# Weight combinations of a seven-product projection on VectorE instead of GpSimd

## The chip, the cores and the metric

The kernel runs on one core of a Trainium2 chip. The metric is the device time of one execution in microseconds (us). The engines that matter are TensorE (PE, matrix products; PEld is its loading of weights), VectorE (DVE), ScalarE (ACT), GpSimd (POOL) and SyncE (SP, which here issues the DMA transfers). Each engine works through its own instructions in a fixed order, and they meet at semaphores.

## What is computed

Two batches of 1024 tokens with 1024 channels pass through four layers: causal attention with rotary positions and an adapter prefix (32 heads of 32), a feed-forward layer with routed low-rank experts, a second attention (8 heads of 16), and the feed-forward layer again. Only the projections of the first attention are touched by the change:

```python
def _L0_attn_a_ref(x, w_attn, w_proj, adapter_wte, gating):
    qkv = jnp.einsum('btc,oc->bto', x, w_attn)
    q, k, v = jnp.split(qkv, 3, axis=-1)
    ...
    q = _apply_rope(q, cos, sin)
    k = _apply_rope(k, cos, sin)
    scores = jnp.einsum('bhqd,bhkd->bhqk', q, k) / jnp.sqrt(jnp.asarray(hd, x.dtype))
    scores = jnp.where(causal, scores, jnp.asarray(-jnp.inf, x.dtype))
    attn = jax.nn.softmax(scores, axis=-1)
    y = jnp.einsum('bhqk,bhkd->bhqd', attn, v)
    ...
x = L0_attn_a_x
x = x + _L0_attn_a_ref(_layernorm(x, axis=-1), L0_attn_a_w_attn, L0_attn_a_w_proj, L0_attn_a_adapter_wte, L0_attn_a_gating)
x = x + _L0_ffn_ref(_layernorm(x, axis=-1), ...)
x = x + _L0_attn_b_ref(_layernorm(x, axis=-1), ...)
x = x + _L0_ffn_ref(_layernorm(x, axis=-1), ...)
```

## The kernel before

**Stages.** Stage A (`stage_a`) holds the first attention for both batches and takes the first half of the time; after it come the output projection, the feed-forward layers and the second attention, which the change leaves alone. In stage A the heads are taken in eight groups of four. `attend` walks through rounds: in each round PE writes one double bank of scores (`sc`, line L304), one double bank of transposed scores (`st`, L372 and L374), products with v (L396), and then a portion of filler work. VectorE finds each row's minimum of the negated scores in a custom instruction with a read of its accumulator (L317), ScalarE forms the exponentials (L325, L485), GpSimd masks the diagonal (L381). The two double banks take turns, so PE's next scores need VectorE to be done with the last ones.

**Filler.** The class `Filler` holds generators of PE work, above all the projections of the coming groups, and puts them between the rounds. It also has a list of chores, small jobs for other engines. After each portion of PE work it runs one chore; `flush` runs all that are left at once. Running a chore means that its instruction is placed at this point of its engine's order. PE and GpSimd follow the order in which the program is written; on VectorE the instructions marked with `keep_in_program_order` do (`pin_sub`, `pin_add` among them).

**Seven products.** For all groups but the first of each batch, `project_blocks` makes k and q of a group with seven block products instead of eight (`seven`), and `values` does the same for v of two groups, half at a time. The rows of the normalized input and of the weights are each cut into two by two blocks. The seven products need sums and differences of blocks:

- of the input, once a batch: `combine` stores three of them in DRAM (`td`, streamed back as `tt`), `combine_first` changes one block in place;
- of the weights, for every set: `factors` makes s1 = w21 + w22, s2 = s1 - w11 and w21 = w11 - w21 (chores, L629), `last_factor` w12 - s2 (chores, L635). Each is 128x512 elements and is done by GpSimd in two pieces of 128x256.

In `seven` the products come in the order 1, 6, 2, 7, 5, 4, 3. Product 6 uses s2, product 7 the changed w21, product 5 s1 and the changed input block, product 3 the last combination. `first` and `settled` are `rotate` for k and q: a shuffle and a product on VectorE (L795, L796), then four instructions on GpSimd (L799, L800). Before product 6 and before product 3 the whole list of chores is flushed. The last combination's chores are put on the list behind product 5.

There are 14 such sets for k and q (groups 1 to 7 of two batches; tiles `wqk`, `s`) and 7 for v (`wv`, `s_v`). A set of k and q is begun at the end of the projection before (`begin`), a set of v in the middle of an even group (`begin_values`, at the `None` that `seven` yields). For the first value set of batch 1 this isn't so: it is begun at the head of `values`, right in front of its own product 1, behind the chores of `combine_first` and of the k and q set of group 1.

Of the kernel before, what the change touches and what calls it, by code (L numbers as in the profile page):

```python
# [21 lines left out]
B, T, C = 2, 1024, 1024  # L22
# [26 lines left out]
class Filler:  # L49
# [10 lines left out]
        self.ahead = 0  # L60
        self.chores = deque()

    def flush(self):
        while self.chores:
            self.chores.popleft()()

    def add(self, gen, gate=None):
        self.gens.append((gen, gate))
# [1 line left out]
    def step(self, cold=True):  # L70
        while self.gens:
            g, gate = at = self.gens[0]
            if gate is not None and gate not in self.done:
                return None
            if not cold and isinstance(g, Dense) and not g.ready:

                g.prepare()
                return None
            try:
                r = next(g)  # L80
            except StopIteration:
                self.gens.remove(at)
                self.ahead = 0
                continue
            if r is WAIT:
                return None
            if r is AHEAD:
                self.ahead += 1
                self.prepare(1)
                continue  # L90
            if isinstance(r, tuple):
                self.done.add(r)
                self.at[r] = self.spent
                continue
            self.spent += r
            if self.chores:
                self.chores.popleft()()
            return r
        return None

# [43 lines left out]
def tile_model(ctx: ExitStack, tc: tile.TileContext, d, out: bass.AP):  # L144
    nc = tc.nc
    pe, dve, act, pool, sp = nc.tensor, nc.vector, nc.scalar, nc.gpsimd, nc.sync
# [3 lines left out]
    fill = Filler()  # L150
# [8 lines left out]
    def block_bank(shape, name, i=0):  # L159
        return ps.tile(shape, F32, tag=pair[i], name=name)  # L160
# [363 lines left out]
    def stage_a(wk, big):  # L524
# [58 lines left out]
        def in_pieces(op):  # L583
            def both(dst, x, y):
                for h in range(0, HF, 2 * P):
                    op(dst[:, h : h + 2 * P], x[:, h : h + 2 * P], y[:, h : h + 2 * P])
            return both

        def pin_sub(*a):
            tc.keep_in_program_order(dve.tensor_sub(*a))  # L590
# [4 lines left out]
        def made(ts, b, i, c, op, x, y):  # L595
            t = ts[i, c] = big.tile([P, HF], F32, tag="tt", name=f"tn{b}_{i}_{c}")
            op(t, x, y)
            sp.dma_start(td[b, i, c], t)

        def combine(b):  # L600

            ts = {}
            for c in range(4):
                b11, b12, b21, b22 = (block(b, i)[:, c, :] for i in (11, 12, 21, 22))
                fill.chores.append(lambda c=c, x=b22, y=b12: made(ts, b, 3, c, pin_sub, x, y))
                fill.chores.append(lambda c=c, y=b11: made(ts, b, 2, c, pin_add, ts[3, c], y))
                fill.chores.append(lambda c=c, y=b21: made(ts, b, 4, c, in_pieces(pool.tensor_sub), ts[2, c], y))

            order = []
            for g in range(NG):  # L610
                order += [2, 3, 4] if g else []
                if g > 1 or b:
                    order += [4] if g % 2 else [2, 3]
            fill.chores.append(lambda: streams.update({b: Stream(b, order)}))

        def combine_first(b):
            for c in range(4):
                t1, b11 = block(b, 12)[:, c, :], block(b, 11)[:, c, :]
                fill.chores.append(lambda t1=t1, b11=b11: in_pieces(pool.tensor_sub)(t1, t1, b11))

        def factors(w, tag, nm):


            s1, s2 = (wk.tile([P, 4, P], F32, tag=tag, name=f"s{i}_{nm}", bufs=2) for i in (1, 2))
            for op, dst, x, y in ((pool.tensor_add, s1, w[21], w[22]), (pool.tensor_sub, s2, s1, w[11]),
                                  (pool.tensor_sub, w[21], w[11], w[21])):
                for c in range(0, 4, 2):
                    cs = slice(c, c + 2)
                    fill.chores.append(lambda op=op, dst=dst, x=x, y=y, cs=cs: op(dst[:, cs], x[:, cs], y[:, cs]))  # L629
            return {1: w[11], 2: w[12], 3: w[12], 4: w[22], 5: s1, 6: s2, 7: w[21]}  # L630

        def last_factor(f):
            for c in range(0, 4, 2):
                cs = slice(c, c + 2)
                fill.chores.append(lambda cs=cs: pool.tensor_sub(f[3][:, cs], f[3][:, cs], f[6][:, cs]))  # L635

        def seven(b, nm, f, mul, shape, c, first, settled):

            right = {1: lambda k: block(b, 11)[:, k, :], 2: lambda k: block(b, 21)[:, k, :], 3: lambda k: block(b, 22)[:, k, :],
                     4: lambda k: streams[b].get(4, k), 5: lambda k: block(b, 12)[:, k, :],
                     6: lambda k: streams[b].get(2, k), 7: lambda k: streams[b].get(3, k)}

            def product(i, dst, start=True, stop=True):
                for k in range(4):
                    yield from mul(dst, f[i][:, k, :], right[i](k), start and k == 0, stop and k == 3)

            x = block_bank(shape, f"x_{nm}")
            yield from product(1, x, stop=False)  # L650
            act.copy(c[22], x)
            fill.flush()
            y = block_bank(shape, f"y6_{nm}", 1)
            yield from product(6, y)
            tc.keep_in_program_order(dve.tensor_add(c[12], c[22], y))
            yield from product(2, x, start=False)
            first(x)
            y = block_bank(shape, f"y7_{nm}", 1)
            yield from product(7, y)
            tc.keep_in_program_order(dve.tensor_add(c[21], c[12], y))  # L660
            yield None
            z = block_bank(shape, f"z_{nm}")
            yield from product(5, z, stop=False)
            last_factor(f)
            tc.keep_in_program_order(dve.tensor_add(c[22], c[21], z))
            settled(22)
            y = block_bank(shape, f"y4_{nm}", 1)
            yield from product(4, y)
            tc.keep_in_program_order(dve.tensor_sub(c[21], c[21], y))
            settled(21)  # L670
            yield True
            fill.flush()
            yield from product(3, z, start=False)
            tc.keep_in_program_order(dve.tensor_add(c[12], c[12], z))
            settled(12)
            pair.rotate(1)
# [151 lines left out]
        def project_first(b, between):  # L828
            wqk = wqk_at[b, 0]
            if b == 0:  # L830
                yield adapter_parts("k0", lambda c: wqk[:, c, 1, :], P)
            else:
                assert next(turnover) is None
            for n in range(2):
                if n == 1:
                    if b == 0:
                        yield from between
                    combine(b)
                xh = xnT[b, n]
                for s, key in ((1, "k"), (0, "q")):  # L840
                    qp = next_bank([P, HF], f"{key}p{b}_{n}")
                    for c in range(NC):
                        mm(qp, lhsT=wqk[:, c, s, :], rhs=xh[:, c, :], start=(c == 0), stop=(c == NC - 1))
                        yield HF * COL
                        if b and n == 0 and c % 2:
                            yield next(turnover)
                    rotate(b, 0, key, n, qp)
                    if b == 0 and n == 0 and key == "k":
                        yield adapter_keys(0)
                yield ("qk", b, 0, n)  # L850
                if b == 0:
                    yield from values_first(n)
            combine_first(b)
# [48 lines left out]
        def values(b, g):  # L902

            e = g - g % 2
            if (b, g) == (1, 0):
                yield from begin_values(b, g)
            i = 0
            for r in st["seven", b, e]:
                if r is None:
                    yield ("v", b, e, 0)  # L910
                    return
                if r is not True:
                    yield r
                    i += 1
                    if i == 4 and b == 0 and g == e:
                        yield adapter_values(g)
            if e + 2 < NG:
                wv_at[b, e + 2] = v_load(b, e + 2)
            elif b == 0:
                wv_at[1, 0] = v_load(1, 0)  # L920
            yield ("v", b, e, 1)
# [512 lines left out]
```

## Time and profile before

| what | value |
|---|---|
| median of 3 runs | 2531.49 us (2529.31 to 2534.36) |
| the profiled execution: its time, its span | 2530.25 us, 2528.5 us |
| mean granted TensorE clock | 0.990 |
| TensorE busy | 2442.0 us (97%) |
| VectorE busy | 1273.5 us (50%) |
| ScalarE busy | 1091.8 us (43%) |
| GpSimd busy | 604.9 us (24%) |
| in stage A from 63 to 1264 us: PE, DVE, ACT, POOL busy | 1148.6, 665.0, 693.4, 444.4 of 1200.8 us |

The page gives sums of busy time, and the span in 40 slices with the share of the full TensorE clock that was granted. The table of waits names for each waiting line the instruction that released it, then the total, the number of times and the longest. A row of the timeline gives start and duration in us, engine, line, operation, tiles written and read, shape and count, and in brackets the idle time ahead of it with its releaser. A row of the windows gives the stretch, its length, busy time and instructions of PE, PEld, DVE, ACT and POOL, then granted clock, DMA share and GB/s. A row of the groups gives line, engine, operation, tiles, shapes and count, then busy us and mean ns of one, then idle time before.

Of the moved work the profile has these groups on GpSimd, 128x256 each: L629 with 28 instructions for each of three combinations of wqk (732 to 737 ns) and 14 for each of wv (730 to 734 ns), L635 with 28 for wqk (783 ns) and 14 for wv (735 ns).

### The profile page before, as it was taken

The numbers are of one execution on the slowest core, as the hardware profiler recorded it, in microseconds if no ns is written. First come the engines' busy times: TensorE is split into PE (matmuls) and PEld (weight loads), VectorE is DVE, ScalarE is ACT, GpSimd is POOL, SyncE is SP. The second block draws the span as 40 slices with busy tenths as digits, with TensorE's granted clock in tenths as the row PEclk, the third lists the DMA queues.
The fourth block names the chain that finished last, engine by engine and source line by source line (L and its number), as shares of the span: only waits on it lengthen the run. The fifth ranks groups of instructions, "written<-read, shape, count | busy, mean of one in ns | idle before, by whom it ended". The sixth has DMA issues, their size and how long they took to land.

```text
span 2528.5 us, 60549 instructions
## 1 busy us (share of the span) xinstructions
PE 2442.0 (97%) x25477; PEld 1101.8 (44%) x25477; DVE 1273.5 (50%) x4036; ACT 1091.8 (43%) x2085; POOL 604.9 (24%) x968
## 2 busy tenths in 40 slices
PE   7989999999989999999999999999999999999999
PEld 4424434444444444445433445566333563333344
DVE  7655555556545565555530014356555765654243
ACT  3336656566545666566642000011344525554300
POOL 1443442333334444233300002100100101111120
PEclk9989999999989999999999999999999999999999
DMA  6622322323323333232322461121000301212121
GB/s 210 208 85 78 103 74 89 98 80 98 126 76 106 94 95 104 82 93 93 109 70 66 156 211 55 50 92 43 34 34 34 126 35 34 93 43 76 51 100 42
DMA packets 142514, 224.35 MB, mean 89 GB/s; under 512 B 12833, under 2 KB 73377, under 8 KB 142241
## 3 DMA queue, kind: packets, MB, share of 16 engines
q1 hardware_dynamic: 142240, 220.48, 26.7%
q8 instruction: 199, 3.26, 0.5%
q14 instruction: 75, 0.61, 0.1%
HBM read 168.01 MB, written 52.43 MB: 87 GB/s over the span
## 4 chain that ended last, share of the span: by engine, by line
PE 83%; DVE 6%; ACT 5%; POOL 3%; issue 2%; DMA 1%; SPq 0%; ACTq 0%; DVEq 0%; POOLq 0%
PE fo_f L203 11%; PE st L374 9%; PE fo_f L205 7%; PE sc L304 7%; PE op L203 6%; PE y_A L396 5%; PE y L205 4%; PE z L205 4%; PE op L205 3%; PE st L372 3%; PE x L205 3%; ACT pr_A L325 2%; PE y_B L396 2%; PE bq L203 2%; PE y_v L205 2%
## 5 line engine op out<-in xcount | busy, mean ns | idle before, releaser
L485 ACT ACTIVATE pt<-st 128x1024 f32<-128x1024 f32 (+1 forms) x418 | 426.4, 1020 | 682.6 <-PE st L374 512.8
L325 ACT ACTIVATE pr_A<-pr_A,nmax_A 128x896 f32<-128x896 f32 (+7 forms) x512 | 389.9, 765 | 58.6 <-DVE nmax_A L317 57.8
L317 DVE CUSTOM_DVE_ANT_0 pr_A<-sc,mask 128x512 f32<-128x512 f32 (+3 forms) x512 | 251.0, 537 | 218.8 <-PE sc L304 125.8
L304 PE MATMUL sc<-kT,qT 32*128 32x512 f32 (+3 forms) x1536 | 329.2, 525 | 11.8 <-DVE nmax_A L317 10.2
L374 PE MATMUL st<-qT,kT 32*128 32x512 f32 (+3 forms) x1536 | 309.9, 490 | 0.0
L221 POOL TENSOR_TENSOR xf<-xf,b_base 128x256 f32<-128x256 f32 x128 | 89.2, 728 | 760.3 <-DVE xn_f L243 457.2
L317 DVE CUSTOM_DVE_ANT_0 pr_A<-sc,mask,part_A 128x512 f32<-128x512 f32 (+1 forms) x256 | 156.5, 648 | 192.3 <-PE sc L304 132.2
L203 PE MATMUL fo_f<-wb,xt_f 128*128 128x512 f32 x558 | 251.3, 593 | 0.4 <-ACT hwT_f L1139 0.4
L205 PE MATMUL fo_f<-wb,xt_f 128*32 128x512 f32 x1864 | 221.9, 595 | 0.0
L381 POOL TENSOR_SCALAR_AFFINE_SELECT pt<-pt 128x256 f32<-128x256 f32 x256 | 99.7, 408 | 483.3 <-ACT pt L485 483.3
L325 ACT ACTIVATE pr_B<-pr_B,nmax_B 128x1024 f32<-128x1024 f32 x128 | 145.6, 1140 | 41.3 <-DVE nmax_B L317 41.1
L396 PE MATMUL y_A<-pt,v 128*32 128x512 f32 (+3 forms) x1536 | 160.3, 500 | 0.2 <-POOL pt L381 0.2
L203 PEld LDWEIGHTS fo_f<-wb,xt_f 128*128 128x128 f32 x558 | 102.9, 192 | 112.8 <-issue 112.2
L304 PE MATMUL sc<-kq,qk 32*128 32x512 f32 x512 | 144.3, 640 | 3.2 <-DVE nmax_B L317 2.8
L203 PE MATMUL op<-wp,yt 128*128 128x512 f32 x338 | 145.7, 592 | 0.0
L374 PE MATMUL st<-rows_B,kq 32*128 32x512 f32 x512 | 144.3, 640 | 0.0
L374 PEld LDWEIGHTS st<-qT,kT 32*128 32x128 f32 x1536 | 134.0, 186 | 16.6 <-issue 11.6
L235 ACT ACTIVATE lv_f<-ve_f 128x1 f32<-128x1 f32 x32 | 6.5, 203 | 309.4 <-DVE ve_f L233 309.4
L372 PE MATMUL st<-rows_A,ones 3*128 3x512 bf16 (+3 forms) x768 | 128.2, 330 | 3.3 <-DVE nmax_A L317 3.3
L317 DVE CUSTOM_DVE_ANT_0 pr_B<-sc,mask,part_B 128x512 f32<-128x512 f32 x128 | 91.2, 747 | 79.7 <-PE sc L304 79.7
L304 PEld LDWEIGHTS sc<-kT,qT 32*128 32x128 f32 x1536 | 113.4, 184 | 28.7 <-DVE nmax_A L317 13.3
L372 PEld LDWEIGHTS <-ones 3*128 3x128 bf16 x768 | 36.4, 91 | 190.9 <-issue 183.5
(274 smaller groups left out, 3743.9 us busy)
## 6 DMA issues: line engine op xcount, KB each, us to landing
tt<-td SPq DMA_DIRECT2D x252, 256.0 KB, 2.8
wqk<-in_w_attnT SPq DMA_DIRECT2D x32, 512.0 KB, 5.1
xf<-x SPq DMA_DIRECT2D x32, 512.0 KB, 3.3
xa<-in_x SPq DMA_DIRECT2D x16, 512.0 KB, 5.9
wv<-in_w_attnT SPq DMA_DIRECT2D x8, 1024.0 KB, 5.4
yd<-ys SPq DMA_DIRECT2D x32, 256.0 KB, 2.7
yt<-yd SPq DMA_DIRECT2D x128, 64.0 KB, 2.0
xp<-in_x SPq DMA_DIRECT2D x32, 256.0 KB, 2.9
```

The lines of the kernel that those rows point to most:

```text
L203: return pe.matmul(out, lhsT=lhsT, rhs=rhs, start=start, stop=stop, skip_group_check=True)
L205: pe.matmul(out[i : i + 32], lhsT=lhsT[:, i : i + 32], rhs=rhs, start=start, stop=stop, skip_group_check=True)
L221: pool.tensor_add(dst[:, i : i + 2 * P], a[:, i : i + 2 * P], b[:, i : i + 2 * P])
L235: act.activation(lv, ve, AF.Ln)
L304: yield w * COL, lambda: pe.matmul(dst[:, o : o + w], lhsT=self.qt[rows, qc : qc + P], rhs=self.kt[rows, c0 : c0 + w], start=True, stop=True)
L317: dve.tensor_tensor_reduce(pr[:, c0 : c0 + w], sc[:, i, o : o + w], m, -self.scale, BIG if c0 == 0 else self.part[:, col], ALU.add, ALU.mi ...
L325: tc.keep_in_program_order(act.activation(pr[:, :nk], pr[:, :nk], AF.Exp, bias=self.nmax[:, col], scale=-1.0, accum_out=self.sums[:, col]))
L372: yield w * COL / 4, lambda: pe.matmul(dst[:, o : o + w], lhsT=ones[three, :], rhs=self.rows[three, off : off + w], start=True, stop=False)
L374: yield w * COL, lambda: pe.matmul(dst[:, o : o + w], lhsT=self.kt[rows, kb * P : (kb + 1) * P], rhs=rhs, start=self.extra, stop=True)
L381: pool.affine_select(out=dg, in_=dg, compare_op=ALU.is_ge, fill=0.0, base=0, pattern=[[0, 2], [1, P]], channel_multiplier=-1)
L396: pe.matmul(self.y[32 * h : 32 * h + 32, off : off + w], lhsT=self.value(h, kb), rhs=pt[h // 2][:, h % 2, o : o + w], start=self.opens, st ...
L485: act.activation(pt[:, :, low_:wide_], st[:, :, low_:wide_], AF.Exp, scale=ts[0][0].scale)
```

## The change

The three combinations of `factors` become single VectorE instructions over 128x512, still as chores. The last combination is no chore any more: it is issued on VectorE right behind the addition that follows product 7, the fourth product. Chores get a key: S for weights of a set, T for the stored input combinations, T1 for the input block that is changed in place. A flush names a key and runs the list up to the last chore of that key: S and T ahead of product 6, T1 ahead of product 5; the flush ahead of product 3 is dropped. The first value set of batch 1 is begun at the start of that batch's first projection.

```diff
-    def flush(self):
-        while self.chores:
-            self.chores.popleft()()
+    def chore(self, key, run):
+        self.chores.append((key, run))
+
+    def flush(self, key):
+
+        while any(k == key for k, _ in self.chores):
+            self.chores.popleft()[1]()
...
         def combine_first(b):
             for c in range(4):
                 t1, b11 = block(b, 12)[:, c, :], block(b, 11)[:, c, :]
-                fill.chores.append(lambda t1=t1, b11=b11: in_pieces(pool.tensor_sub)(t1, t1, b11))
+                fill.chore(("T1", b), lambda t1=t1, b11=b11: in_pieces(pool.tensor_sub)(t1, t1, b11))
...
             s1, s2 = (wk.tile([P, 4, P], F32, tag=tag, name=f"s{i}_{nm}", bufs=2) for i in (1, 2))
-            for op, dst, x, y in ((pool.tensor_add, s1, w[21], w[22]), (pool.tensor_sub, s2, s1, w[11]),
-                                  (pool.tensor_sub, w[21], w[11], w[21])):
-                for c in range(0, 4, 2):
-                    cs = slice(c, c + 2)
-                    fill.chores.append(lambda op=op, dst=dst, x=x, y=y, cs=cs: op(dst[:, cs], x[:, cs], y[:, cs]))
+            for op, dst, x, y in ((pin_add, s1, w[21], w[22]), (pin_sub, s2, s1, w[11]), (pin_sub, w[21], w[11], w[21])):
+                fill.chore(("S", nm), lambda op=op, dst=dst, x=x, y=y: op(dst, x, y))
             return {1: w[11], 2: w[12], 3: w[12], 4: w[22], 5: s1, 6: s2, 7: w[21]}
-
-        def last_factor(f):
-            for c in range(0, 4, 2):
-                cs = slice(c, c + 2)
-                fill.chores.append(lambda cs=cs: pool.tensor_sub(f[3][:, cs], f[3][:, cs], f[6][:, cs]))
...
             act.copy(c[22], x)
-            fill.flush()
+            fill.flush(("S", nm))
+            fill.flush(("T", b))
             y = block_bank(shape, f"y6_{nm}", 1)
...
             tc.keep_in_program_order(dve.tensor_add(c[21], c[12], y))
+            pin_sub(f[3], f[3], f[6])
             yield None
+            fill.flush(("T1", b))
             z = block_bank(shape, f"z_{nm}")
             yield from product(5, z, stop=False)
-            last_factor(f)
             tc.keep_in_program_order(dve.tensor_add(c[22], c[21], z))
...
             yield True
-            fill.flush()
             yield from product(3, z, start=False)
...
             else:
                 assert next(turnover) is None
+                yield from begin_values(b, 0)
...
             e = g - g % 2
-            if (b, g) == (1, 0):
-                yield from begin_values(b, g)
```

## The prediction

> **What bounds the kernel now.** I read the page first: busy shares, granted clock by slice, the chain that ended last.
>
> ```profile
> PE 2442.0 (97%) x25477; PEld 1101.8 (44%) x25477; DVE 1273.5 (50%) x4036; ACT 1091.8 (43%) x2085; POOL 604.9 (24%) x968
> PEclk9989999999989999999999999999999999999999
> PE 83%; DVE 6%; ACT 5%; POOL 3%; issue 2%; DMA 1%; SPq 0%; ACTq 0%; DVEq 0%; POOLq 0%
> ```
>
> TensorE is the bound: 2528.5 - 2442.0 = 86.5 us idle in the whole span. The kernel can gain only where PE stands still or runs below full clock. PE's own waits come next.
>
> ```profile
> PE z L205 <- POOL wqk L635: 15.9, 7, 6.3
> PE y_v L205 <- POOL s_v L629: 11.8, 1, 11.8
> PE sc L304 <- DVE nmax_A L317: 10.2, 9, 2.3
> PE z_v L205 <- POOL wv L635: 0.9, 3, 0.4
> ```
>
> The first, second and fourth are products waiting for a combination of weights that GpSimd makes: 15.9 + 11.8 + 0.9 = 28.6 us in 11 waits, the largest group. All lie in stage A, the first 1264 us. The third is the price of a late VectorE, which the change loads further.
>
> PE in order of time gives the places. Three z waits are small (0.35 each); the others begin to run again at 145.19 (6.31), 197.84 (2.14), 360.80 (3.18), 519.25 (3.18), and y_v at 711.29 (11.81). The two outer ones:
>
> ```profile
> 139.00 0.68 DVE L665 TENSOR_TENSOR qT<-qT,z 128x512 f32<-128x512 f32 x1
> 144.42 1.40 POOL L635 TENSOR_TENSOR wqk<-wqk,s 128x256 f32<-128x256 f32 x2
> 145.19 5.30 PE L205 MATMUL z<-xnT,wqk 128*32 128x512 f32 x32 [6.31 <-POOL wqk L635]
> 148.07 0.72 POOL L800 TENSOR_TENSOR qT<-qT,qr 128x256 f32<-128x256 f32 x1
> 151.72 1.14 PE L304 MATMUL sc<-kT,qT 32*128 32x128 f32 x8
> ...
> 710.49 1.44 POOL L629 TENSOR_TENSOR s_v<-s_v,wv 128x256 f32<-128x256 f32 x2
> 711.29 1.94 PE L205 MATMUL y_v<-s_v,tt 128*32 128x128 f32 x32 [11.81 <-POOL s_v L629]
> ```
>
> At 144.42 the subtraction stands on GpSimd behind a rotation that waited for VectorE. At 710.49 six pieces of another set (705 to 709) and eight of combine_first stand ahead. Neither is slow arithmetic; both are places in a queue.
>
> A stop also costs clock. Windows of 5 to 7 us from the restart:
>
> ```profile
> 145.19:150.19 5.00, 5.00 (x32) 1.26 (x36) 0.00 (x0) 0.00 (x0) 3.45 (x5) 0.66 0.00 0
> 360.80:367.80 7.00, 7.00 (x34) 1.54 (x36) 1.31 (x4) 1.03 (x1) 3.44 (x5) 0.55 0.01 2
> 519.25:524.25 5.00, 5.00 (x30) 1.18 (x34) 1.31 (x4) 1.02 (x1) 3.45 (x5) 0.66 0.00 0
> 711.29:716.29 5.00, 5.00 (x81) 3.61 (x85) 1.00 (x3) 0.78 (x1) 2.01 (x3) 0.61 0.17 52
> 1085.91:1090.91 5.00, 5.00 (x94) 3.44 (x98) 2.42 (x11) 4.21 (x14) 0.77 (x2) 0.66 0.03 9
> ```
>
> The sixth value is the granted clock, PE being busy throughout: lost are 5 x 0.34 = 1.7, 7 x 0.45 = 3.15, 1.7, 5 x 0.39 = 1.95 and 1.7 us. After 197.84 it was 1.00.
>
> **The change, part by part.** *Removed:* 21 sets (14 of wqk, 7 of wv) of 8 GpSimd pieces, 168 x about 0.73 = 122 us of POOL. *Added:* 84 VectorE instructions. The order of the two programs' instructions shows PE and ACT unchanged, VectorE with 84 insertions and nothing else, SP with one xn load ahead of one tt load; that xn load waits for earlier transfers alone, so 0. Duration of one: the rows nearest are L796 with both inputs in SBUF (0.732 mean of 28), and L593 next to busy GpSimd (0.820 of 8):
>
> ```profile
> L796 DVE TENSOR_TENSOR qT<-qT,cos 128x512 f32<-128x512 f32 x28 | 20.5, 732 | 1.0
> L593 DVE TENSOR_TENSOR tn<-tn,xnT 128x512 f32<-128x512 f32 x8 | 6.6, 820 | 1.1 <-DMA td<-tn 1.0
> ```
>
> I take 0.73, as 122 us of GpSimd partners vanish: 84 x 0.73 = 61 us, in a stage where VectorE is busy 665 of 1201 us.
>
> *Gain, stop by stop.* (A) 145.19: 6.31 + 1.7 = 8.0 are on offer, not all to be had. Product 3 adds to the bank that VectorE reads until 139.68 (L665); PE stopped at 138.88, so 0.8 stays. Then scores need the rotated q, ready at 148.79 now. Without the 1.4 us of L635 it is ready at about 147.4, while PE would ask from 144.6: some 2.5 us of new wait, the next late thing. Left 4.7. (B) 197.84: 2.1. (C) 360.80: 3.2 + 3.15 = 6.3. (D) 519.25: 3.2 + 1.7 = 4.9; at B, C, D the next score bank is free before PE would come. (E) 711.29: 11.8 + 1.95 = 13.8; its set moves to the start of the batch's first projection and needs no GpSimd. (F) three z waits and three z_v waits, 1.1 + 0.9 = 2.0. (H) 1085.91: here GpSimd's sets held VectorE's tiny instructions (L342 to L347 took 2.94 us in sum, against 1.16 at 452.9 to 454.3), scores waited 2.08, and clock was lost: 1.8 + 1.7 = 3.5. Sum 4.7 + 2.1 + 6.3 + 4.9 + 13.8 + 2.0 + 3.5 = 37.3 us.
>
> The subtraction right behind product 7's addition is ready 9 to 37 us before product 3 (at 130.6 for 145.19), under products 5 and 4, so no new wait there; without that cover PE would wait its 0.73.
>
> *Cost.* VectorE runs in order: an insertion delays the score minima behind it (L317), whose end frees the bank PE's next scores need. I set each of the 84 at its place in the trace of before and let idle time in front of score arrivals absorb it. Most vanish in idle stretches of 1 to 3 us. Seven delays exceed PE's slack: 0.62 at 113.3, 0.48 at 294.8, 0.16, 1.40 at 457.8, 0.19, 0.57 at 856.1, 0.54 at 929.3; together 4.0, of which I count 3.4, since PE is late at 113 anyway. That is because the first set (second group of heads) is now built behind minima ending at 110.05: s1, a small product, s2 give 111.7, but product 6 stood ready at 109.38: 2.3 us of new wait, and by the pattern above perhaps 1.7 of clock. Queued behind are its rows of scores and all of PE. The moved value set sits right behind the addition ending at 639.77; its load is issued at 633.61, transfers of wv land in 5.0 to 8.0 us, so it waits 0 to 1.8, then takes 2.2. Behind it are two transposed copies; 0.3 us for PE (0 to 2). The move itself issues no DMA and no matmul in this batch. Splitting the flushes leaves GpSimd's other work in the same order: 0; below nothing is excluded, as that order is read, not guessed. Last, PE running 35 us earlier will meet waits now covered; four big stops at 0.7 (the small waits in the list) give 3.0. Sum 3.4 + 2.3 + 1.7 + 0.3 + 3.0 = 10.7.
>
> Net 37.3 - 10.7 = 26.6 us off the profiled execution of 2530.25 (span 2528.5). The median lies 1.2 above it: 2531.5 - 26.6 = 2505.
>
> *A rule against it.* The Trainium skill, "SBUF — State Buffer", section "Who interferes with whom", says that a VectorE instruction with two SBUF inputs and a GpSimd instruction that reads SBUF cannot run together: the second is blocked until the first is done. All 84 are of that kind. Were each caught behind a full 0.73 piece, it would take 0.68 + 0.73 = 1.41 us; the same placing then gives 33 score waits, 31.0 us in sum. The rows say 0.73 and 0.82: caught about one time in ten. The row is taken, the rule bounds the cost. Stage A at 1060 to 1090 shows that the lock is real (H).
>
> *And one on the clock.* "TensorE: Matmul & The Clock Gate", section "Part 1: The HAM clock gate (the "warmup" mystery)", has the clock fall after an idle window of about 3.4 us. By it only A and E would regain clock (3.65 us). The trace shows half clock behind 3.18 (twice) and even 2.08 us, so I count 10.2 us in all, less what A keeps.
>
> **The rivals.** (1) *The stop is handed on.* At A, C, D, E (29.7 us) half goes to the next late thing, as at A: for it speaks the rotation chain; against it, free banks at C and D. Instead of 3.0 it costs 14.9: net 14.7, 2517. Chance 0.17. (2) *VectorE becomes the late engine*: the lock makes its insertions long, at L317, on the path to the score banks. At 1.41 each: 31.0, plus half clock behind eight waits over 1.4 (8 x 1.7 = 13.6), plus 3.5 + 1.7 for the first set, 0.3 and 3.0, less 37.3: +15.8, 2547. At 1.05 the placing gives 11.9 and 3.4 of clock; it turns to a loss near 1.2 us each. Against it: L796's rows and less GpSimd work. Chance 0.05. (3) *It doesn't do what it says*: products still stand still because banks or tiles, not weights, were last; then within 0.2%, 2529. The wait rows name GpSimd with its instruction ending just before PE starts: 0.07. (4) *Nothing is lost on VectorE*: 37.3 in full, 2494. Chance 0.08. The forecast keeps 0.63.
>
> **Range and chances.** 2494 to 2518 spans the forecast, (4)'s end and (1). A measurement can tell about 0.2%, 5 us, from no change. Faster 0.63 + 0.17 + 0.08 = 0.88, same 0.07, slower 0.05.
>
> **What would show it.** PE's waits on POOL for wqk, wv, s_v gone; POOL near 483 busy, DVE near 1335; clock 1.00 after the places of C, D, E; L205 waiting about 2.3 us for a VectorE s near 109; a wait on qT near 145; scores waiting for L317 in sum 10 to 16. It is wrong if the inserted rows average over 1 us, or if L317's waits exceed 30.

## The result and the profile after

Over ten runs each the changed kernel took 2520.2 us (2513.3 to 2524.8) and the kernel before 2534.25 us (2529.3 to 2537.7). The ratio is 0.9949, 95% interval 0.9937 to 0.9962: 13 us off by the ratio and 14 by the medians, where the forecast had 26.6, and the time lies 2 us above the stated range. (The forecast's base, three runs of the kernel before, lay 2.8 us below the median of ten.) The profiled execution of the changed kernel took 2524.32 us, span 2522.6 us.

The page of the changed kernel (line numbers are shifted by the edit: L317 is now L321, L304 is L308, L372 is L376, L796 is L793, L799 and L800 are L796 and L797; the combinations are L594 and L597):

```profile
PE 2444.0 (97%) x25477; PEld 1107.0 (44%) x25477; DVE 1334.8 (53%) x4120; ACT 1092.2 (43%) x2085; POOL 501.0 (20%) x800
...
PEclk9999999999999999999999999999999999999999
...
PE 84%; DVE 7%; ACT 5%; DMA 2%; issue 1%; POOL 1%; SPq 0%; DVEq 0%; ACTq 0%; POOLq 0%
```

VectorE has its 84 instructions and 61 us more, as forecast, but this sum hides something: the 84 take 70.8 us, 0.84 in the mean. Busy time counts stretches in which two records overlap once, and the older instructions have become 3.5 us shorter in all. GpSimd has 501.0 us instead of the forecast 483: the rotation's pieces (kr and qr 0.89 and 0.96 us in the mean instead of 0.85 and 0.93, kT 0.84 instead of 0.75) have become longer, 11 of these 18 us. What PE waits for now (total, times, longest):

```profile
PE sc L308 <- DVE nmax_A L321: 13.6, 11, 3.6
PE st L376 <- DVE nmax_A L321: 10.8, 11, 2.4
PE sc L308 <- POOL qT L797: 4.8, 4, 1.9
...
PE y L209 <- DVE s L594: 2.0, 1, 2.0
...
PE y_A L400 <- POOL pt L385: 1.3, 1, 1.3
```

Two rows of before that belong beside these:

```profile
PE st L372 <- DVE nmax_A L317: 3.3, 3, 1.8
PE sc L304 <- POOL qT L800: 1.4, 2, 0.7
```

The stops on GpSimd's wqk, s_v and wv (28.6 us) are gone, all of them. In their place the waits on VectorE's score minima have risen from 10.2 + 3.3 = 13.5 to 13.6 + 10.8 = 24.4 us, product 6 waits 2.0 for its s2, and 3.4 us more go to the rotated q. The groups of the new instructions show a first reason (the last numbers are busy us, mean ns of one, idle before):

```profile
L597 DVE TENSOR_TENSOR s<-wqk 128x512 f32<-128x512 f32 x14 | 14.8, 1057 | 0.0
...
L594 DVE TENSOR_TENSOR s<-s,wqk 128x512 f32<-128x512 f32 x14 | 13.7, 978 | 0.2
L594 DVE TENSOR_TENSOR wqk<-wqk 128x512 f32<-128x512 f32 x14 | 13.3, 947 | 0.0
...
L594 DVE TENSOR_TENSOR wqk<-wqk,s 128x512 f32<-128x512 f32 x14 | 9.9, 704 | 0.0
...
L594 DVE TENSOR_TENSOR s_v<-s_v,wv 128x512 f32<-128x512 f32 x7 | 4.8, 690 | 0.2
```

The last combination and the value sets take 0.68 to 0.70 us. The three combinations of a wqk set take 1.06, 0.98 and 0.95 us in the mean; 28 of the 42 are over 0.8. One set in the timeline, VectorE, GpSimd and PE in order of time:

```profile
837.75 0.69 DVE L793 TENSOR_TENSOR kT<-kT,cos 128x512 f32<-128x512 f32 x1
837.80 1.23 POOL L796 TENSOR_TENSOR kr<-kr,sin 128x256 f32<-128x256 f32 x1 [3.38 <-DVE kr L792]
838.36 1.22 DVE L597 TENSOR_TENSOR s<-wqk 128x512 f32<-128x512 f32 x1
...
839.11 1.05 POOL L797 TENSOR_TENSOR kT<-kT,kr 128x256 f32<-128x256 f32 x1
...
839.61 1.10 DVE L594 TENSOR_TENSOR s<-s,wqk 128x512 f32<-128x512 f32 x1
...
840.12 1.18 POOL L796 TENSOR_TENSOR kr<-kr,sin 128x256 f32<-128x256 f32 x1
...
840.63 1.22 DVE L594 TENSOR_TENSOR wqk<-wqk 128x512 f32<-128x512 f32 x1
841.38 1.05 POOL L797 TENSOR_TENSOR kT<-kT,kr 128x256 f32<-128x256 f32 x1
...
841.77 0.74 DVE L321 CUSTOM_DVE_ANT_0 pr_A<-sc,mask,part_A 128x512 f32<-128x512 f32 x1
...
843.25 0.39 PE L376 MATMUL st<-rows_A,ones 3*128 3x512 bf16 x2 [1.69 <-DVE nmax_A L321]
```

The set stands right behind the rotation of k on VectorE, that is, exactly while GpSimd does its four pieces of that rotation. The two engines take turns: each instruction behind the first starts while the other engine's is running and takes 0.3 to 0.5 us longer than alone. The minima that PE needs start at 841.77. In the kernel before, the same place reads:

```profile
852.85 0.69 DVE L796 TENSOR_TENSOR kT<-kT,cos 128x512 f32<-128x512 f32 x1
852.89 1.23 POOL L799 TENSOR_TENSOR kr<-kr,sin 128x256 f32<-128x256 f32 x1 [3.94 <-DVE kr L795]
...
854.70 0.75 DVE L317 CUSTOM_DVE_ANT_0 pr_A<-sc,mask,part_A 128x512 f32<-128x512 f32 x1 [1.17 <-PE sc L304]
...
856.59 0.39 PE L372 MATMUL st<-rows_A,ones 3*128 3x512 bf16 x2
```

There VectorE is free for 1.2 us before the scores arrive, the minima start as soon as they are there, and PE doesn't wait. The second line holds what the prediction overlooked: the 0.69 us instruction started 0.04 us ahead of GpSimd's piece, and it is the piece that paid (1.23 us; 0.73 when alone).

Aligning PE's instructions in the two traces, the changed kernel is 11.6 us ahead at the end of stage A (1264 us); behind it, where the change has no instruction, this execution loses 5.7 us again, 5.3 of it at half clock by the record of the granted clock, in places (1938, 1969 and 2416 us) where the other has none. The half clock has chance in it ahead of the change too. PE's wait of 2.65 us at 47 us, before any moved instruction, stands in all 14 traces kept; behind it 3 of them (before, e8, e10) show no half clock, 4 show 3.4 us of it and 7 (the changed kernel among them) 6.8 us. So the changed kernel is 3.2 us behind at 63 us for no reason of the change. One trace against one trace is good for the place of a wait, not for the last 5 us of a sum; those are left to the medians and ratios.

### The profile page after: what moved, and what is told of

Its sections match the earlier page's. It is cut to its first block, busy times and chain, and to the rows that moved or that the text cites. A ratio compares the mean times of both kernels' runs of the same rounds, so it can differ in the third digit from the quotient of the medians.

```text
span 2522.6 us, 60430 instructions
## 1 busy us (share of the span) xinstructions
PE 2444.0 (97%) x25477; PEld 1107.0 (44%) x25477; DVE 1334.8 (53%) x4120; ACT 1092.2 (43%) x2085; POOL 501.0 (20%) x800
## 4 chain that ended last, share of the span: by engine, by line
PE 84%; DVE 7%; ACT 5%; DMA 2%; issue 1%; POOL 1%; SPq 0%; DVEq 0%; ACTq 0%; POOLq 0%
PE fo_f L207 11%; PE st L378 9%; PE fo_f L209 8%; PE sc L308 7%; PE op L207 6%; PE y_A L400 5%; PE y L209 5%; PE z L209 3%; PE op L209 3%; PE st L376 3%; PE x L209 3%; ACT pr_A L329 2%; PE y_B L400 2%; PE bq L207 2%; PE y_v L209 2%; DVE pr_A L321 2%
## 5 line engine op out<-in xcount | busy, mean ns | idle before, releaser
L308 PE MATMUL sc<-kT,qT 32*128 32x512 f32 (+3 forms) x1536 | 329.3, 525 | 18.5 <-DVE nmax_A L321 13.6
L321 DVE CUSTOM_DVE_ANT_0 pr_A<-sc,mask 128x512 f32<-128x512 f32 (+3 forms) x512 | 250.9, 536 | 180.5 <-PE sc L308 94.4
L321 DVE CUSTOM_DVE_ANT_0 pr_A<-sc,mask,part_A 128x512 f32<-128x512 f32 (+1 forms) x256 | 156.3, 647 | 162.4 <-PE sc L308 114.8
L308 PE MATMUL sc<-kq,qk 32*128 32x512 f32 x512 | 145.1, 643 | 3.5 <-DVE nmax_B L321 3.2
L378 PEld LDWEIGHTS st<-qT,kT 32*128 32x128 f32 x1536 | 133.9, 186 | 16.7 <-issue 11.6
L376 PE MATMUL st<-rows_A,ones 3*128 3x512 bf16 (+3 forms) x768 | 128.0, 330 | 10.8 <-DVE nmax_A L321 10.8
L321 DVE CUSTOM_DVE_ANT_0 pr_B<-sc,mask,part_B 128x512 f32<-128x512 f32 x128 | 91.1, 747 | 81.3 <-PE sc L308 81.2
L308 PEld LDWEIGHTS sc<-kT,qT 32*128 32x128 f32 x1536 | 113.9, 185 | 35.1 <-DVE nmax_A L321 17.3
L376 PEld LDWEIGHTS <-ones 3*128 3x128 bf16 x768 | 37.1, 91 | 197.2 <-issue 189.7
```

The costliest lines, as they stand in the source:

```text
L308: yield w * COL, lambda: pe.matmul(dst[:, o : o + w], lhsT=self.qt[rows, qc : qc + P], rhs=self.kt[rows, c0 : c0 + w], start=True, stop=True)
L321: dve.tensor_tensor_reduce(pr[:, c0 : c0 + w], sc[:, i, o : o + w], m, -self.scale, BIG if c0 == 0 else self.part[:, col], ALU.add, ALU.mi ...
L376: yield w * COL / 4, lambda: pe.matmul(dst[:, o : o + w], lhsT=ones[three, :], rhs=self.rows[three, off : off + w], start=True, stop=False)
L378: yield w * COL, lambda: pe.matmul(dst[:, o : o + w], lhsT=self.kt[rows, kb * P : (kb + 1) * P], rhs=rhs, start=self.extra, stop=True)
```

## The experiments

Theory 1: the wqk sets are dear because they lie beside GpSimd's rotation of k; each instruction is held by GpSimd's pieces, the minima behind them come late, and PE waits. Theory 2: any work put in front of the minima costs this, held or not. Theory 3: the difference is one of the clock's phase and of stops handed on to the rotation of q. All kernels were timed against the kernel before on the same chip; the ratio is to those runs. The chip is not the same for all kernels, so between two kernels a difference of medians and one of ratios can part by up to 3 us. "Minima" is the sum of the two waits on nmax_A; "wqk set" the mean of one of the three combinations on VectorE, in us.

| kernel | median us | ratio, 95% interval | minima | wqk set |
|---|---|---|---|---|
| before | 2534.25 | 1 | 13.5 | GpSimd |
| changed | 2520.2 | 0.9949 (0.9937, 0.9962) | 24.4 | 0.99 |
| e1: wqk sets on GpSimd | 2503.9 | 0.9877 (0.9862, 0.9892) | 13.6 | GpSimd |
| e2: wqk sets as one-input shuffles | 2511.6 | 0.9909 (0.9895, 0.9923) | 17.4 | 0.74 |
| e3: wqk sets later | 2508.6 | 0.9893 (0.9877, 0.9908) | 12.6 | 0.70 |
| e4: all sets on GpSimd | 2507.4 | 0.9890 (0.9874, 0.9906) | 13.9 | GpSimd |
| e5: first set on GpSimd | 2519.6 | 0.9939 (0.9925, 0.9952) | 25.9 | 0.99 |
| e6: last subtraction alone | 2519.0 | 0.9938 (0.9924, 0.9952) | 14.1 | GpSimd |
| e7: early value set alone | 2522.8 | 0.9957 (0.9944, 0.9969) | 13.6 | GpSimd |
| e8: first on GpSimd, rest later | 2503.4 | 0.9875 (0.9860, 0.9890) | 13.9 | 0.70 |
| e9: e8, GpSimd put beside the sets | 2501.7 | 0.9875 (0.9860, 0.9890) | 12.2 | 0.75 |
| e10: e8, GpSimd put behind the sets | 2503.2 | 0.9881 (0.9866, 0.9895) | 13.1 | 0.70 |
| e11: first two on GpSimd, rest later | 2498.8 | 0.9856 (0.9840, 0.9873) | 12.5 | 0.70 |
| e12: first two on GpSimd, rest as changed | 2516.8 | 0.9923 (0.9909, 0.9936) | 25.2 | 1.02 |

**e1, the wqk sets back on GpSimd.** Here and below `on_pool` puts each of the three on the list as two pieces of 128x256 for GpSimd, as before the change; `pool_ops` and `dve_ops` are the three operations on GpSimd and on VectorE.

```diff
-            for op, dst, x, y in ((pin_add, s1, w[21], w[22]), (pin_sub, s2, s1, w[11]), (pin_sub, w[21], w[11], w[21])):
-                fill.chore(("S", nm), lambda op=op, dst=dst, x=x, y=y: op(dst, x, y))
+            def on_pool(ops):
+                for op, dst, x, y in ops:
+                    for c in range(0, 4, 2):
+                        cs = slice(c, c + 2)
+                        fill.chore(("S", nm), lambda op=op, dst=dst, x=x, y=y, cs=cs: op(dst[:, cs], x[:, cs], y[:, cs]))
...
+            if tag == "sa":
+                on_pool(pool_ops)
+            else:
+                for op, dst, x, y in dve_ops:
+                    fill.chore(("S", nm), lambda op=op, dst=dst, x=x, y=y: op(dst, x, y))
```

> From the changed kernel, the three combinations of each of the 14 wqk sets go back to GpSimd in halves; the last subtraction (right behind product 7), the value sets on VectorE, the keyed flushes and the early value set stay. Theory 1 (the three VectorE instructions of a wqk set fall on GpSimd's rotation pieces, take about 1.1 to 1.2 us instead of 0.69 and push the score minima): scores' and st's waits on the minima fall from 24.4 to 14 to 17 us, the stop on s near 114 goes, no stop on POOL wqk comes back but perhaps one of about 2 us near 1086; 24.4 - 15.5 = 9 us of waits, 2.3 near 114 and some 3 us of clock less, 3 us for GpSimd's hold on VectorE's small instructions back: 2520 - 11 = about 2509 (2506 to 2514). Theory 2 (any work put on VectorE there costs the same, caught or not): the same here, about 2509. Theory 3 (the difference is the clock's phase and the stops handed on to the rotation): 2517 to 2521.

It gave 2503.9, below the expected 2506 to 2514: 16 us off the changed kernel. The minima are back at 13.6 us and the stop on s is gone. So the wqk sets on VectorE cost some 16 us (18 by the ratios), and theory 3 is not the main cause. Between theories 1 and 2 this run can't tell.

**e2, the same work with one input.** This is the run that tells theories 1 and 2 apart: the number, size and place of the VectorE instructions stay, and only their second SBUF input goes (for the 14 wqk sets; the value sets stay). The shuffle only copies one block, so this kernel leaves the weights uncombined and its output means nothing; it serves for the time alone. Each shuffle brings a small mask instruction of 0.015 us along.

```diff
-            for op, dst, x, y in ((pin_add, s1, w[21], w[22]), (pin_sub, s2, s1, w[11]), (pin_sub, w[21], w[11], w[21])):
+            def one_input(dst, x, y):
+                tc.keep_in_program_order(dve.stream_shuffle(dst, x, list(range(32))))
+
+            pick = (one_input, one_input, one_input) if tag == "sa" else (pin_add, pin_sub, pin_sub)
+            for op, (dst, x, y) in zip(pick, ((s1, w[21], w[22]), (s2, s1, w[11]), (w[21], w[11], w[21]))):
```

> From the changed kernel, the three combinations of each wqk set are replaced by a VectorE shuffle of the same size and place with one input (the weights are then not combined, so the output is not the reference's). The number of VectorE instructions and their order stay. Theory 1: each takes about 0.73 us instead of 1.0 to 1.2, waits on the minima fall from 24.4 to about 17 us, and with 2 or 3 us of clock the time is about 2511 (2509 to 2514). Theory 2: waits stay at 22 to 25 us and the time within 2 us of 2520.

Its groups and its waits on the minima:

```profile
L630 DVE STREAM_SHUFFLE wqk<-wqk 128x512 f32<-128x512 f32 x14 | 10.5, 750 | 0.0
...
L630 DVE STREAM_SHUFFLE s<-wqk 128x512 f32<-128x512 f32 x14 | 10.2, 732 | 0.0
```
```profile
PE sc L308 <- DVE nmax_A L321: 12.1, 11, 2.8
PE st L376 <- DVE nmax_A L321: 5.3, 7, 2.4
```

Beside the same GpSimd pieces each takes 0.73 to 0.75 us, the minima fall to 17.4 (expected: about 17), and the time by 8.6 us to 2511.6. The two intervals do not meet. So some half of what e1 gains is the hold itself. Theory 2 alone is excluded; that another 3 to 8 us (to e3, e1 and e8 below) hang on the place itself is not. The run also stands for the kernel that the prediction had in mind, with 0.74 us for each of these instructions: its waits on the minima are 17.4 - 13.5 = 3.9 us above before, and it gains 23 us.

**e3, the sets later.** Twelve empty chores stand in front of each wqk set, so that it lies behind the rotation.

```diff
+            if tag == "sa":
+                for _ in range(12):
+                    fill.chore(("S", nm), lambda: None)
```

> From the changed kernel, the first combination of each wqk set comes twelve fill steps later, so that the set lies behind GpSimd's rotation of k and not beside it. Theory 1: the three instructions take 0.70 to 0.80 us each, waits on the minima fall to about 17 us, time about 2512 (2510 to 2515). Theory 2: durations may fall, but waits stay above 21 us and the time at 2517 to 2521, since the minima behind them are pushed as before.

The instructions take 0.69, 0.72 and 0.71 us, the minima 12.6 us, less than before the change, the time is 2508.6. This is against a theory 2 for which 42 more instructions on VectorE cost the same anywhere: in this place they cost the minima nothing. It does not tell the hold from the place, since it changes both; e2 does. What is left is new: product 6 waits 3.9 us for s2 in two places (at 113 and 164 us), since there the set has no time to be late.

**e4, all sets on GpSimd.** Only the last subtraction (L594) is on VectorE.

```diff
-            for op, dst, x, y in ((pin_add, s1, w[21], w[22]), (pin_sub, s2, s1, w[11]), (pin_sub, w[21], w[11], w[21])):
-                fill.chore(("S", nm), lambda op=op, dst=dst, x=x, y=y: op(dst, x, y))
...
+            on_pool(pool_ops)
```

> From the changed kernel, all three-combination sets (wqk and values) are on GpSimd in halves; on VectorE there is only the last subtraction right behind product 7, with the keyed flushes and the early value set. Theory 1 and 2: like the version with only the wqk sets on GpSimd, about 2509 (2506 to 2514), as the value sets were caught in no instance (0.69 us) and pushed the minima little. If the value sets on VectorE are what took away a stop (711 us), this one is 3 to 12 us slower than that version.

2507.4, as expected. Whether the value sets are better on VectorE (e1, 2503.9) stays open: the intervals overlap.

**e5, only the first set on GpSimd.**

```diff
+            if nm == "0_1":
+                on_pool(pool_ops)
+            else:
+                for op, dst, x, y in dve_ops:
+                    fill.chore(("S", nm), lambda op=op, dst=dst, x=x, y=y: op(dst, x, y))
```

> From the changed kernel, only the first set of all (second group of heads of the first batch) goes back to GpSimd in halves; the other 13 wqk sets stay on VectorE beside GpSimd's rotation. The stop on s near 114 (2.0 us) and the half clock behind it (1.6 us) go: about 3.6 us off 2520, 2516 (2514 to 2518), by either theory. If the gain of the version with all wqk sets on GpSimd (16 us) were mainly this one stop, it would come to 2508 or less.

A miss: the stop near 114 is gone from the trace, the time isn't lower by the expected 3.6 us but by 0.6 (2.5 by the ratios), which can't be told from nothing. The other 13 sets are as dear as before (1.09, 0.92 and 0.97 us). In its profile this execution was 5 us behind before by 101 us, ahead of the set (half clock behind the wait at 47 us, and a wait of 3.6 us on the minima at 101), so it can't decide what the stop was worth.

**e6 and e7, the two other parts by themselves.** In e6 the kernel before gets `pin_sub(f[3], f[3], f[6])` behind product 7's addition in place of `last_factor`. In e7 the changed kernel has all combinations on GpSimd, and keeps the early value set and the keyed flushes.

```diff
             tc.keep_in_program_order(dve.tensor_add(c[21], c[12], y))
+            pin_sub(f[3], f[3], f[6])
...
-            last_factor(f)
```

> From the kernel before, one edit alone: the last subtraction of every set is one VectorE instruction right behind product 7's addition; the three combinations stay on GpSimd, the value set is not moved. The forecast's terms for it are A 4.7, B 2.1, C 6.3, D 4.9 and 1.1 of the small waits, 19.1 us; its 14 + 7 instructions cost VectorE nothing that shows. If these hold: 2534 - 19 = 2515 (2512 to 2519), with the stop near 711 (about 12 us) still there. If stops are handed on to the next late thing by half: 2524.

> From the changed kernel, all combinations are back on GpSimd, the last subtraction too, in halves behind product 5 as before; only the early value set of the second batch and the keyed flushes stay. The forecast's term E is 13.8 us: 2534 - 14 = 2520 (2517 to 2524), and the stops at 145, 198, 361 and 519 are there again. Handed on by half: 2527.

The first line is from the waits of e6, the second from those of e7:

```profile
PE y_v L205 <- POOL s_v L629: 11.8, 1, 11.8
```
```profile
PE z L209 <- POOL wqk L672: 15.8, 7, 6.3
```

Each took away its own stops and left the other's. e6 gained 0.0062 of 2533.3, 15.7 us (19 expected), e7 0.0043, 10.9 us (14 expected). Their sum, 26.6, is what both together gain in e4 (0.0110, 27.9). These parts are right in mechanism and, by the middle of their intervals, about a fifth smaller than forecast.

**e8, the first set on GpSimd, the other 13 later.**

The edit is that of e11 below with `"0_1"` alone.

> From the changed kernel, the first set on GpSimd, and the other 13 wqk sets on VectorE but twelve fill steps later, behind GpSimd's rotation. Theory 1 (only the neighbourhood of GpSimd's rotation makes the sets dear): each instruction takes about 0.70 us, the time is that of the version with all wqk sets on GpSimd, 2504 (2502 to 2507). Theory 2 (work put on VectorE costs in itself): 4 us or more above it, 2508 to 2512.

2503.4, where theory 1 said 2504 and theory 2 2508 to 2512. All work but one set is on VectorE, and the kernel is as fast as with the wqk sets on GpSimd. So work on VectorE costs nothing in itself that can be measured; like e3, this moves the sets away from GpSimd's pieces and from the minima at once.

**e9 and e10, the hold put back.** From e8, GpSimd adds a zero tile to a weight block of each set, in two pieces: in e9 as soon as the set's first instruction is done, in e10 when its third is (there the condition is i == 2 and the tile w[21]).

```diff
+            def beside(t):
+                for c in range(0, 4, 2):
+                    h = t[:, c : c + 2]
+                    pool.tensor_add(h, h, mask[:, : 2 * P].rearrange("p (i q) -> p i q", i=2))
+
+            def run(i):
+                op, dst, x, y = dve_ops[i]
+                op(dst, x, y)
+                if i == 0:
+                    beside(w[22])
```

> From the version with the first set on GpSimd and the rest later on VectorE (ratio 0.9875 to before), GpSimd gets two additions of zero, 128x256, to w22 of each of the 20 sets on VectorE; they may start when the first instruction of the set is done, so they lie beside its second and third. The values do not change. Theory 1: the first instruction of each set stays at 0.69 us, the second and third take 1.0 to 1.25 instead of 0.69; 40 instructions by 0.4 = 16 us more of VectorE, of which scores wait some 4 to 8 with the clock behind them: ratio 0.989 to 0.991. Theory 2 (no lock, only the order on VectorE): durations stay at 0.69 and the ratio at 0.9875.

> The control of the version with GpSimd beside: the same two additions of zero for each set, but to the tile that the set's third instruction writes, so that they start when the set is done. Theory 1: all three instructions of a set stay at 0.69 to 0.72 us; ratio within 0.0015 of 0.9875. Theory 2: the same durations; a time above that by 0.002 or more would mean that the GpSimd work itself costs, not its place beside the set.

Half a miss, and a useful one. Where the pieces did meet a set, in e9:

```profile
313.80 0.68 DVE L597 TENSOR_TENSOR s<-wqk 128x512 f32<-128x512 f32 x1
...
314.51 0.69 DVE L594 TENSOR_TENSOR s<-s,wqk 128x512 f32<-128x512 f32 x1
...
314.56 1.23 POOL L648 TENSOR_TENSOR wqk<-wqk,mask 128x256 f32<-128x256 f32 x1 [0.92 <-DVE s L597]
...
315.12 1.22 DVE L594 TENSOR_TENSOR wqk<-wqk 128x512 f32<-128x512 f32 x1
```

The second instruction began 0.05 us ahead of the piece and keeps its 0.69; the piece pays (1.23). The third begins behind the piece and pays (1.22). So the hold is real and follows from who starts first. But in most sets VectorE was the first or a score minimum lay between: 18 of the 40 pieces paid (1.15 to 1.24 us), while of the 20 third instructions 8 are over 0.8 us, two of which are so in e8 too. VectorE's combinations grew by 59.5 - 56.6 = 2.9 us and not by 16, and the time is that of e8. In e10 GpSimd's pieces take 0.73 us and the third instructions 0.71 and 0.68, as in e8. So 2.9 us of hold in places where VectorE has room cost nothing that can be measured; what 16 us would cost there wasn't tried.

**e11 and e12, and the fastest version.** In e11 the second set too is on GpSimd; the other 12 stand later on VectorE. e12 has the same two sets on GpSimd and the other 12 where the change has them (the diff without the three lines of the empty chores).

```diff
+            if nm in ("0_1", "0_2"):
+                on_pool(pool_ops)
+            else:
+                if tag == "sa":
+                    for _ in range(12):
+                        fill.chore(("S", nm), lambda: None)
+                for op, dst, x, y in dve_ops:
+                    fill.chore(("S", nm), lambda op=op, dst=dst, x=x, y=y: op(dst, x, y))
```

> From the version with the first set on GpSimd and the rest later on VectorE, the second set (third group of heads) goes to GpSimd too, as its delayed place lies right in front of product 6, which waited 1.9 us for it near 161. That stop and perhaps 1.7 us of half clock go: ratio 0.9863 (0.985 to 0.9875) by both theories; GpSimd's rotation of q ahead of it may hand the stop on, then 0.9875.

> From the changed kernel, the first two sets on GpSimd as in the fastest version (2498.8 us, ratio 0.9856), the other 12 wqk sets on VectorE at once, beside GpSimd's rotation, as the change has them. So it differs from the fastest version only in the place of 12 sets. Theory 1: the instructions of these sets take about 1.1 us in the median again, waits on the minima are 20 us or more, ratio 0.993 (0.9915 to 0.9945), some 18 us slower than the fastest version. If the first two sets were what held the gain back, it comes to 0.988 or less.

e11 is the fastest, 2498.8 us, 35 us below before. The waits on the minima, first of e11, then of e12:

```profile
PE sc L308 <- DVE nmax_A L321: 8.6, 9, 2.0
...
PE st L376 <- DVE nmax_A L321: 3.9, 3, 2.4
```
```profile
PE sc L308 <- DVE nmax_A L321: 14.0, 11, 3.6
PE st L376 <- DVE nmax_A L321: 11.2, 11, 2.4
```

The two differ in nothing but the place of 12 sets, and that is 2516.8 - 2498.8 = 18 us (17 by the ratios), with intervals far apart. The two traces show it place by place: within 3 us of the end of nine of these sets e12's PE stops for the minima, 11.0 us in all, the longest 3.65 (at 456 us), 1.72 (1067) and 1.68 (840); of these nine e11 has one that is over 0.3 us, 1.38 at 452. The first two sets are the difference between the changed kernel and e12: 3.4 us by the medians, 6.6 by the ratios, whose intervals just fail to meet.

## Why the prediction was wrong

The sign and the mechanism of the gain were right; the price was not. The step that failed is in the paragraph on what is added and under the rule: "I take 0.73, as 122 us of GpSimd partners vanish", and "The rows say 0.73 and 0.82: caught about one time in ten. The row is taken, the rule bounds the cost." Of the 42 instructions of the wqk sets 28 were over 0.8 us, two in three, and the mean was 0.99. So the delays of the minima, of which the prediction counted 3.4 us, came to 10.9 us of waits and some clock. Two things were wrong with the row. First, L796 is a row of winners: it begins just ahead of GpSimd's first rotation piece, so it has 0.69 to 0.73 us, and the loser stands in another row (L799: 0.85 us in the mean for k, where a piece alone takes 0.73; 15 of the 64 took 1.17 to 1.25).

```profile
L796 DVE TENSOR_TENSOR kT<-kT,cos 128x512 f32<-128x512 f32 x14 | 10.1, 723 | 0.4
...
L799 POOL TENSOR_TENSOR kr<-kr,sin 128x256 f32<-128x256 f32 x64 | 54.3, 848 | 106.1 <-DVE kr L795 86.9 <-DVE r_a L241 17.5 <-DVE m_A L343 1.6
```

Second, the partners that vanish are not the ones beside the new place: the order of the instructions put each wqk set right behind L795 and L796, where four rotation pieces are always at hand. The Trainium skill, "SBUF — State Buffer", section "Who interferes with whom", was the better guide in this place: it says that the one that starts second is blocked until the first is done. The trace agrees on who pays, though most of the caught instructions (24 of the 28) took 1.10 to 1.23 us and not the 1.41 that the prediction worked out as the worst case.

The prediction's own sum shows what was missing. It says that at 1.05 us each the same placing gives 11.9 us of waits and 3.4 of clock. The wqk sets took 0.99, the waits on the minima rose by 24.4 - 13.5 = 10.9. With 11.9 + 3.4 for the 3.4 that were counted, the net gain is 26.6 - 11.9 = 14.7 us, and 2534.25 - 14.7 = 2519.6: the other terms nearly close the sum. The placing itself was sound: at 0.74 us each (e2) the waits rose by 3.9 us, near the 3.4 that were counted for 0.73. That the sum closes to a microsecond is partly luck: e6 and e7 gained 26.6 us where their terms had 32.9, or 29.9 with the 3.0 for waits now covered.

The signs that the prediction named did not show the error. VectorE's busy time came out as forecast, the inserted rows average 0.84 us, below the 1 that was to be the alarm, and the scores (sc) wait 13.6 us, inside the 10 to 16; the 10.8 us of the transposed scores (st) were not in that list. Rival 2 named this mechanism, and priced it at 1.41 each with a net loss; its turning point, 1.2 us each, was not reached.

What the place cost can be read a second way. At the end of stage A the changed kernel is 11.6 us ahead of before and e11 30.3, 18.7 more; the first two sets are in this too. The waits on the minima account for 24.4 - 12.5 = 11.9 of them, the stop on s for 2.0, the waits on the rotated q for 4.8 - 4.1 = 0.7, the wait of y_A on GpSimd's mask for 1.3 - 0.2 = 1.1, and the time lost to half clock, from the record of the granted clock, for 15.4 - 12.0 = 3.4: 19.1 in all, about half a microsecond more than the traces differ.

Point by point, from PE's instructions aligned in the two traces:

- *A:* 7.1 us were regained at 145, and then 3.6 lost at the rotated q (1.93 and 1.44 us, at 153 and 155) and about 1.8 of clock behind it. Forecast 4.7, kept 1.7. The next late thing was named rightly, and its size too: without a set beside it these two waits are 1.28 and 1.44 us (e11), where the forecast had 2.5 in sum. Its clock was not counted. Most of the other 0.65 us comes from the hold: a piece of q's rotation starts with the first instruction of a set and takes 1.25 us (in e11 the same piece takes 0.72). A little later the two traces part by 3.4 us the other way, and that is luck: behind a wait of 1.83 us that both have (158.89 in before, 163.74 in the changed kernel) before shows 6.8 us of half clock and the changed kernel none.

```profile
151.86 0.68 DVE L597 TENSOR_TENSOR s<-wqk 128x512 f32<-128x512 f32 x1
151.86 1.25 POOL L797 TENSOR_TENSOR qT<-qT,qr 128x256 f32<-128x256 f32 x1
...
153.17 0.49 PE L308 MATMUL sc<-kT,qT 32*128 32x128 f32 x4 [1.93 <-POOL qT L797]
```

- *B, C, D, E:* 2.3, 6.4, 5.0, 13.9 against 2.1, 6.3, 4.9, 13.8. Right, clock included.
- *F:* the three z and three z_v waits on GpSimd are gone; each of the six places gains 0.36 to 0.54 us, 2.9 in sum against 2.0.
- *H:* 3.5 forecast. The six small instructions do run at 0.17 to 0.32 us now, but with the set of that group, held from 1065.3 to 1068.8, in front of the minima, PE waits 1.38 us at 1070, and the wait of 2.08 us is still there (1.98 at 1075.6). With the set out of the way the term is there: between 900 and 1100 us e11 gains 4.0 us on before, e1 with its sets on GpSimd 0.6.
- *First set and product 6:* 2.3 and 1.7 forecast, 1.95 us at 114.33 and 3.4 us at half clock behind it (the 0.50 behind the five engines in the row of the window), 1.7. Right in the trace; e5 could not show it in the time.

```profile
115.00:118.40 3.40, 3.40 (x22) 1.14 (x22) 0.41 (x3) 0.47 (x1) 0.00 (x0) 0.50 0.82 295
```

- *Waits now covered, 3.0:* not to be read from these traces. Three half-clock stretches that before doesn't show, near 238, 613 and 770 us, cost 1.7 us each. They lie behind stops that before has too (at 237.5, 617.5 and 785.1 us), two of them of the same length, and are there in e1 and e4 as well, so they don't come from the sets.

Not settled: what the first two sets are worth by themselves in the changed kernel (0.6 us in e5, 3.4 in e12, 5 between e3 and e8 by the medians; 2.5, 6.6 and 4.6 by the ratios), and how the 3 to 8 us between e2 and the later places divide between VectorE's order and GpSimd's.

## What to carry to other kernels

When work is moved to an engine, its duration is not to be read from a row of the same form but from the neighbours at its new place: take the order of the instructions, see what the partner engine does in those microseconds, and look for the row of the one that starts second. A hold that an engine pays where it has room costs little (2.9 us of it in e9 could not be measured); one in front of a result that the bounding engine waits for is passed on, and the same instructions twelve steps later were worth 17 to 18 us. And a change of three parts is worth timing part by part: two parts here gave 27 us, and the third took half of it away.

## What the runs showed of the hardware

In this kernel VectorE's combinations with two SBUF inputs and GpSimd's two-input pieces hold each other, but less than in full: caught, a 128x512 VectorE instruction mostly took 1.10 to 1.23 us instead of 0.69, a 128x256 piece 1.05 to 1.25 instead of 0.73. In the timeline above four pieces and four VectorE instructions, 4 x 0.73 + 4 x 0.69 = 5.7 us of work, filled 837.75 to 842.43, 4.7 us. In the timelines shown the one that started first, by as little as 0.04 us, kept its time. A one-input shuffle of the same size beside the same pieces took 0.77 us at most (0.73 to 0.75 in the mean). The granted clock fell to one half around stops of TensorE, in the changed kernel mostly behind waits of 1.4 to 3.65 us (once, at 770, behind two of 0.7), in stretches of 3.4 us or two to four times that (13.7 us around the stop of 11.8 us in before). The same wait does not always bring it: behind the wait of 2.65 us at 47 us the 14 traces show 0, 3.4 or 6.8 us of half clock, and a stop of 2.0 us at 607 us in e8 has none, where the changed kernel's at 611.75 has 3.4.
